# Routing of the second expert layer issued in two steps, its results scaled in a fixed place, and a table preload in one norm: a sequence model of four layers on one core

## The chip, the cores and the metric

One Trainium2 chip, of which the program uses one core. The metric is the time on the device in microseconds (us) for one execution of the whole program. The kernel before took 1866.34 us, the median of three runs (1865.36 to 1867.81).

## The reference

The input is x, 8 sequences of 256 tokens with 128 channels. Four layers, each with a token mixer and a feed-forward part, each followed by a residual and a layer norm:

- layer 0: a gated linear recurrence, then two blocks of local attention;
- layer 1: a selective state-space scan, then 32 experts, of which each token takes one;
- layer 2: two rounds of 16-head attention over chunks of each sequence, each with a small feed-forward part, then 8 experts, of which each token takes two, beside a common expert that all tokens take;
- layer 3: 16-head causal attention with a decay, then a linear layer with ternary weights.

The change touches the expert part of layer 2 and its seams to what stands before and behind it. Its reference, shortened:

```python
logits = rmsnorm(x) @ router_w.T
probs = softmax(logits)
topk_p, topk_i = top_k(probs, 2)
rw = topk_p / sum(topk_p)                      # gates of a token's two experts
sel = one_hot(topk_i, E).sum(1)
...                                            # first 320 tokens of each expert, in token order
gate = silu(einsum('ech,ehi->eci', xg, rg))
up = einsum('ech,ehi->eci', xg, ru)
eout = einsum('eci,eih->ech', gate * up, rd)   # weighted by rw and added back to the tokens
...
shared = silu(x @ sg) * (x @ su) @ sd          # the common expert, 1024 wide
return shared + routed
```

Behind it stands x = layernorm(x + that).

## The kernel before

Activations lie with the 128 channels on the partitions and the 2048 tokens along the free axis. The program is a row of stages: rglru, local_mamba, moe1, chunked, moe2, typed. Nearly every product goes through one helper, `mm`, so TensorE's instructions in the profile mostly name L394, and one has to tell them apart by their tiles.

**chunked** (L1343) computes the attention of layer 2. Each of the 8 sequences is a generator, `one_sequence` (L1394), that issues a piece of work and yields two guesses: how long TensorE will be busy with it, and how long its results then take. `on_pe` (L277) keeps three such generators alive and always continues the one whose guess says that it is ready first. So the order in which instructions are written is that of this small planner; it is fixed when the program is built, and each engine runs its own instructions in that order (the framework may still move an instruction ahead of others of its engine where nothing forbids it; `issue_after`, L396, fixes an order without adding a wait). The products of a stream carry the names kps (keys), vps (values), sc (scores), pt (transposed scores) and out.

At its end each sequence computes its logits lg for 8 experts and calls `route2` (L1014). This takes Ln and Exp for the norm's factor (L1024, L1025); finds the two best experts with VectorE's compares and maxima (L1030 to L1042, result sel); counts on TensorE, in products named cum, how many earlier tokens chose the same expert (with msk, a triangle of ones, and onesb, all ones); turns counts into places (L1050 to L1056); writes the token's row to its two places in DRAM by four indirect DMAs on GpSimd (`scatter`, L1081, issue at L1083); and computes the gates from an Exp of the difference of the two maxima (L1074 to L1079).

**moe2** (L1460) begins with `rows_of` (L1097): five loads of the placed rows from DRAM, on the queues of SyncE and ScalarE, each behind all scatters. Then comes `shared(0)`, the common expert for the first 512 tokens: eight chunks of a gate product pg, an up product pu, Silu (L1485), a multiplication on VectorE (L1486, tile sh) and a down product that adds to acc. pg and pu share two PSUM banks, sh has two buffers. The rows are transposed (bt), and the 8 experts run over 320 places each; results go to DRAM (ybuf). 32 gathers (`gather`, L1115, issue at L1117) bring the two rows of every group of 128 tokens back; GpSimd issues them. `results(b)` (L1523) weighs them with their gates (two operations on VectorE per group, L1529 and L1530), transposes them, adds the common expert's part and runs the layer norm. The calls stand as follows: shared(1); then shared(2) and shared(3), and between their chunks results(0), the first inputs of typed, and results(1). The results of sequences 2 to 7 are written in typed.

**A layer norm** in steps (L426 to L456) takes a mean product, a subtraction, Square on ScalarE (L448), a variance product, Ln (L453), Exp (L454) and a multiplication. Silu, Ln and Exp need tables in ScalarE; `exp_ln` (L414) loads a table that serves Ln and Exp both. Where the program asks for nothing, the compiler puts a table load ahead of a function that the present table lacks.

**typed** (L1697) runs the attention of layer 3 over 48 units, six per sequence; a queue `side` holds work to be put between units: the inputs of later sequences, their results, and the norms and linear layer behind the attention. Its softmax (L1650) is a maximum on VectorE (L1656), Exp on ScalarE (L1661), a reciprocal (L1663) and a multiplication on GpSimd (L1664).

Of the kernel before, what the change touches and what calls it, by code (L numbers as in the profile page):

```python
# [15 lines left out]
AF = mybir.ActivationFunctionType  # L16
# [280 lines left out]
class _Kernel:  # L297
# [128 lines left out]
    def layernorm_steps(self, pool, src, dst, eps=EPS, tag="ln", steps=False):  # L426

        nc = self.nc
        n = src.shape[-1]
        if not steps and n <= S:  # L430

            ps = self.psum(name="ln")
            xc, var = ps[:, 0:n], ps[:, S : S + n]
            self.mm(xc, self.centre, src)
            sq = pool.tile([P, n], F32, tag=tag + "sq", name="ln_sq", bufs=2)
            nc.scalar.activation(sq, xc, AF.Square)
            self.mm(var, self.mean, sq)
            rs = pool.tile([P, n], F32, tag=tag + "rs", name="ln_rs", bufs=2)
            nc.scalar.activation(rs, var, AF.Ln, bias=eps)
            nc.scalar.activation(rs, rs, AF.Exp, scale=-0.5)  # L440
            nc.vector.tensor_mul(dst, xc, rs)
            return
        mean = self.psum(name="ln_mean")[:, :n]
        self.mm(mean, self.mean, src)
        xc = pool.tile([P, n], F32, tag=tag + "xc", name="ln_xc")
        nc.vector.tensor_sub(xc, src, mean)
        sq = pool.tile([P, n], F32, tag=tag + "sq", name="ln_sq")
        nc.scalar.activation(sq, xc, AF.Square)  # L448
        yield
        var = self.psum(name="ln_var")[:, :n]  # L450
        self.mm(var, self.mean, sq)
        rs = pool.tile([P, n], F32, tag=tag + "rs", name="ln_rs")
        nc.scalar.activation(rs, var, AF.Ln, bias=eps)  # L453
        nc.scalar.activation(rs, rs, AF.Exp, scale=-0.5)  # L454
        yield
        nc.vector.tensor_mul(dst, xc, rs)  # L456

# [556 lines left out]
    def route2(self, b, z, work, small):  # L1014


        nc = self.nc
        E, CAP = 8, 320
        ts = slice(2 * b, 2 * b + 2)
        lg = self.lg2[:, ts]  # L1020
        four = small.tile([P, 7, 2, 2], F32, tag="four", name="four", bufs=2)
        mx, ix, sl, pos, sc, ok = (four[:, i] for i in range(6))
        rs = four[:, 6, 0]
        nc.scalar.activation(rs, self.ssq[:, ts], AF.Ln, scale=1.0 / P, bias=float(np.finfo(np.float32).eps))  # L1024
        nc.scalar.activation(rs, rs, AF.Exp, scale=-0.5)  # L1025
        shp = [P, 2, E]
        each = lambda a: a.unsqueeze(2).to_broadcast(shp)
        io = self.c("iota8").unsqueeze(1).to_broadcast(shp)
        oh = small.tile([P, 2, 2, E], F32, tag="oh", name="oh", bufs=2)
        nc.vector.tensor_tensor(lg, lg, each(rs), ALU.mult)  # L1030
        for k in range(2):

            o = oh[:, k]
            nc.vector.tensor_reduce(mx[:, k], lg, AX.X, ALU.max)
            nc.vector.tensor_tensor(o, lg, each(mx[:, k]), ALU.is_equal)
            nc.vector.tensor_tensor(o, o, io, ALU.mult)
            nc.vector.tensor_reduce(ix[:, k], o, AX.X, ALU.min)
            nc.vector.tensor_tensor(o, io, each(ix[:, k]), ALU.is_equal)
            if k == 0:
                nc.vector.scalar_tensor_tensor(lg, o, NEG, lg, ALU.mult, ALU.add)  # L1040
        sel = small.tile([P, 2, E], BF, tag="sel", name="sel", bufs=2)
        nc.vector.tensor_tensor(sel, oh[:, 0], oh[:, 1], ALU.add)  # L1042

        cum = self.psum("M", "cum")[:, 0 : 2 * E].rearrange("p (t e) -> p t e", e=E)
        self.mm(cum, self.m("upto"), sel, True, False)
        if b:
            self.mm(cum, self.onesb, self.sum2.unsqueeze(1).to_broadcast(shp), False, False)
        self.mm(cum[:, 1, :], self.onesb, sel[:, 0, :], False, True)
        nc.vector.tensor_scalar(sl, ix, float(CAP), float(E * CAP - 1), ALU.mult, ALU.add)
        nc.vector.tensor_tensor(oh, oh, cum.unsqueeze(1).to_broadcast([P, 2, 2, E]), ALU.mult)  # L1050
        nc.vector.tensor_reduce(pos, oh, AX.X, ALU.add)

        nc.vector.tensor_scalar(sc, pos, float(CAP), 100000.0, ALU.is_gt, ALU.mult)
        nc.vector.tensor_add(sl, sl, pos)
        nc.vector.tensor_add(sc, sc, sl)
        placed = nc.vector.tensor_copy(self.put2[:, :, ts], sc)  # L1056
        for t in range(2):
            for k in range(2):
                self.scatter(1, z[:, t, :], self.put2[:, k, 2 * b + t : 2 * b + t + 1])
        if b < B - 1:  # L1060
            with nc.allow_low_precision("whole numbers to 16"):
                for t in range(2):
                    if b or t:
                        nc.vector.tensor_add(self.sum2, self.sum2, sel[:, t, :])
                    else:
                        nc.vector.tensor_copy(self.sum2, sel[:, t, :])

        i = nc.vector.tensor_scalar(sl, sl, float(E * CAP - 1), None, ALU.min)
        self.issue_after([i], placed)
        nc.vector.tensor_copy(self.get2[:, :, ts], sl)  # L1070
        nc.vector.tensor_scalar(ok, pos, float(CAP), None, ALU.is_le)
        g = self.gate2[:, :, ts]
        nc.vector.tensor_sub(sc[:, 1], mx[:, 1], mx[:, 0])
        nc.scalar.activation(sc[:, 1], sc[:, 1], AF.Exp)  # L1074
        nc.vector.tensor_scalar(sc[:, 0], sc[:, 1], 1.0, None, ALU.add)
        nc.vector.reciprocal(sc[:, 0], sc[:, 0])
        nc.vector.tensor_mul(g[:, 0], sc[:, 0], ok[:, 0])
        nc.vector.tensor_mul(sc[:, 1], sc[:, 1], sc[:, 0])
        nc.vector.tensor_mul(g[:, 1], sc[:, 1], ok[:, 1])  # L1079
# [263 lines left out]
    def chunked(self):  # L1343
# [7 lines left out]
        with (  # L1351
# [42 lines left out]
            def one_sequence(b):  # L1394
# [35 lines left out]
                self.logits(b, y, self.w1[:, 866:874], self.lg2[:, 2 * b : 2 * b + 2, :])  # L1430
                assert self.routed == b
                self.routed = b + 1
                self.route2(b, z, work, small)
                yield 0.3, 0.0

            self.routed = 0
            on_pe([one_sequence(b) for b in range(B)], 3, [self.typed_weights(prep)])
# [22 lines left out]
    def moe2(self):  # L1460
# [9 lines left out]
        with (  # L1470
            tc.tile_pool(reuse_waits="tile", name="m2", bufs=1) as one,
            tc.tile_pool(reuse_waits="tile", name="m2w", bufs=2) as work,
        ):
            bt, group = self.rows_of(one, 1)
            ss = []

            def shared(i):
                cs = bass.ts(i, 512)
                acc = self.psum("S", "acc")
                for c in range(8):  # L1480
                    pg, pu = self.psum("A", "pg"), self.psum("A", "pu")
                    self.mm(pg, gu[:, 0, c * P : (c + 1) * P], x[:, cs])
                    self.mm(pu, gu[:, 1, c * P : (c + 1) * P], x[:, cs])
                    h = work.tile([P, 512], F32, tag="sh", name="sh")
                    nc.scalar.activation(h, pg, AF.Silu)  # L1485
                    nc.vector.tensor_mul(h, h, pu)  # L1486
                    self.mm(acc, down[:, c * P : (c + 1) * P], h, c == 0, c == 7)
                    yield
                s = keep.tile([P, 512], F32, name=f"s{i}")
                nc.vector.tensor_add(s, acc, x[:, cs])  # L1490
                ss.append(s)


            for _ in shared(0):
                pass
            ybuf = self.dram.tile([E * CAP, P], F32, name="ybuf2")
            groups = 0
# [25 lines left out]
            def results(b, work):  # L1523

                ps = self.psum("M", "back")
                for j in range(2):
                    t = 2 * b + j
                    r1, r2 = got[t]
                    nc.vector.tensor_scalar(r1, r1, self.gate2[:, 0, t : t + 1], None, ALU.mult)  # L1529
                    nc.vector.scalar_tensor_tensor(r1, r2, self.gate2[:, 1, t : t + 1], r1, ALU.mult, ALU.add)  # L1530
                    nc.tensor.transpose(ps[:, j * P : (j + 1) * P], r1, self.ident)
                s = work.tile([P, S], F32, tag="s", name="s")
                nc.vector.tensor_add(s, ss[b // 2][:, b % 2 * S : (b % 2 + 1) * S], ps[:, 0:S])
                yield
                yield from self.layernorm_steps(work, s, y[:, bass.ts(b, S)], steps=True)

            self.results = results
            for _ in shared(1):
                pass
            self.x = y  # L1540
            first = chain(results(0, self.ty), self.typed_before(0), results(1, self.ty))
            for i in (2, 3):
                for _ in shared(i):
                    next(first, None)
            for _ in first:
                pass
            self.exp_ln()


    def ternary_weights(self, pool, out):  # L1550
# [99 lines left out]
    def typed_softmax(self, unit, sc, work, small):  # L1650
# [9 lines left out]
        for i in reversed(range(n)):  # L1660
            nc.scalar.activation(e[:, i, :], sc[:, i, :], AF.Exp, bias=nm[:, i : i + 1], accum_out=sm[:, i : i + 1])  # L1661
        rc = small.tile([P, n], F32, tag="rc", name="rc")
        nc.vector.reciprocal(rc, sm)  # L1663
        nc.gpsimd.tensor_tensor(e, e, rc.unsqueeze(2).to_broadcast([P, n, keys]), ALU.mult)  # L1664
        return e

# [30 lines left out]
    def typed(self):  # L1697
# [21 lines left out]

        units = [(b, u) for b in range(B) for u in [(0, 0, 4), (0, 4, 8)] + [(1, r, r + 2) for r in range(0, 8, 2)]]  # L1720
        n = len(units)
        side = deque([before(1)])
        scs, es, o = {}, {}, None


# [66 lines left out]
```

## Time and profile before

| | |
|---|---|
| median of three runs | 1866.34 us |
| the profiled execution | 1891.69 us |
| its span, first to last instruction | 1889.9 us |
| mean granted TensorE clock | 0.916 of full |
| TensorE busy | 1575.9 us |
| VectorE busy | 1089.7 us |
| ScalarE busy | 1029.9 us |
| GpSimd busy | 564.0 us |

The profiled execution is 25.35 us above the median of the others. The stages that matter here, on the axis of its span: chunked's sequences up to about 1440 us, shared(0) from 1443 us, the experts, the gathers from 1539.7 to 1579.5 us, shared(2) and (3) from 1584.6 to 1634.5 us, and typed from 1635 us to the end.

How to read the lines. A group or timeline line names the source line, the engine, the operation, the tiles (output, then inputs), the shapes and how many instructions; then come busy time and mean ns in a group, or start and duration in us in a timeline. The bracket at the end of a timeline line is how long the engine had been idle before the instruction, and what ended that. "remote" or "another core or an unknown queue" means that no recorded event was found that ended the wait. Products are pipelined and their ends are modelled.

Two rows of slices, each 1/40 of the span, give the picture: the busy tenths of TensorE and its granted clock.

```profile
PE   3678877888888767677679999999987987999997
PEclk7789999989998898788789999999997998999999
```

A slice is 47.2 us. Counted from 1, slice 31 (1417 to 1465 us) holds the end of chunked and the start of shared(0), slice 34 (1559 to 1606 us) the end of the gathers; both stand at 7.

### The profile page before, as it was taken

To read this page: it belongs to the slowest core of one execution; us is meant where nothing else is said; L and a number is where in the kernel's file an instruction comes from. 1 tells how busy PE (TensorE), PEld (TensorE's weight loads), DVE (VectorE), ACT (ScalarE), POOL (GpSimd) and SP (SyncE) were. 2 spreads that over 40 slices of the span, in tenths; PEclk is the share of its full clock that TensorE was granted. 3 is DMA by queue.
4 is the path that set the end of the run, shared out by engine and by line. 5 is a ranking of instruction groups with operands and counts; after the bars stand their busy time and mean duration, and the time that the engine had idled before them with its cause. 6 is when DMAs were issued, how large, how long until landed. Compare 5 with 4: busy or idle time off the path is not lost.

```text
span 1889.9 us, 28445 instructions
## 1 busy us (share of the span) xinstructions
PE 1575.9 (83%) x10810; PEld 950.7 (50%) x10810; DVE 1089.7 (58%) x2018; ACT 1029.9 (54%) x2703; POOL 564.0 (30%) x493
## 2 busy tenths in 40 slices
PE   3678877888888767677679999999987987999997
PEld 2344544544454434344456676665653643466564
DVE  5734567786878686688434544457543223466664
ACT  4557777776876876455135444444432222466654
POOL 1324452515261413311320201111111034255462
PEclk7789999989998898788789999999997998999999
DMA  4000012121212122175410000000101210000000
GB/s 173 1 1 1 1 35 56 35 56 35 56 35 56 35 56 58 43 224 167 134 48 2 8 6 7 6 5 5 36 2 29 81 52 24 1 4 4 7 4 9
DMA packets 58330, 75.51 MB, mean 40 GB/s; under 512 B 5869, under 2 KB 35237, under 8 KB 57169
## 3 DMA queue, kind: packets, MB, share of 16 engines
q1 hardware_dynamic: 52864, 67.57, 12.3%
q0 software_dynamic: 3216, 5.07, 0.9%
q8 instruction: 85, 1.39, 0.3%
q10 hardware_dynamic: 2112, 1.05, 0.2%
q14 instruction: 53, 0.43, 0.1%
HBM read 65.46 MB, written 9.71 MB: 40 GB/s over the span
## 4 chain that ended last, share of the span: by engine, by line
PE 52%; DVE 18%; ACT 11%; POOL 7%; issue 7%; DMA 3%; another core or an unknown queue 1%; SPq 0%; POOLq 0%; DVEq 0%; ACTq 0%
PE sc L394 7%; PE vps L394 6%; PE kps L394 5%; PE pt L475 4%; PE out L394 4%; DVE hs L789 3%; PE o L394 3%; ACT e L647 3%; PE pu L394 3%; PE pg L394 3%; DVE hs L790 2%; DVE hs L787 2%; PE y L394 2%; PE hps L394 2%; PE py L394 2%
## 5 line engine op out<-in xcount | busy, mean ns | idle before, releaser
L394 PE MATMUL y<-hs,ident 128*128 128x512 f32 x256 | 148.1, 709 | 40.6 <-DVE hs L790 40.6
L789 DVE TENSOR_TENSOR_SCAN hs<-da,hs 128x1024 f32<-128x1024 f32 x64 | 148.8, 2334 | 3.8 <-ACT da L785 3.3
L475 PE MATMUL pt<-ident,e 128*128 128x128 f32 x768 | 125.0, 289 | 28.3 <-POOL e L652 18.1
L1661 ACT ACTIVATE e<-sc,nm 128x128 f32<-128x128 f32 (+1 forms) x256 | 104.3, 425 | 60.4 <-DVE nm L1656 59.7
L652 POOL TENSOR_TENSOR e<-e,rc 128x1024 f32<-128x1024 f32 x32 | 72.2, 2255 | 203.4 <-DVE rc L651 203.3
L785 ACT ACTIVATE da<-d,na 128x255 f32<-128x255 f32 x256 | 112.4, 504 | 36.7 <-DVE hs L789 19.3
L647 ACT ACTIVATE e<-sc,nm,rn 128x128 f32<-128x128 f32 x256 | 113.5, 464 | 25.1 <-DVE nm L642 25.0
L475 PEld LDWEIGHTS pt<-ident,e 128*128 128x128 f32 x768 | 89.7, 146 | 73.6 <-POOL e L652 25.3
L1293 POOL TENSOR_TENSOR e<-e,rc 128x512 f32<-128x512 f32 x32 | 33.6, 1051 | 303.8 <-DVE rc L1292 181.0
L1664 POOL TENSOR_TENSOR e<-e,rc 128x1024 f32<-128x1024 f32 x48 | 91.5, 1908 | 89.0 <-DVE rc L1663 86.1
L599 POOL TENSOR_TENSOR t<-t,t 128x512 f32<-128x512 f32 x64 | 89.1, 1392 | 95.3 <-DVE t L586 86.7
L787 DVE TENSOR_TENSOR hs<-u,bc 128x1024 f32<-128x1024 f32 x64 | 87.0, 1368 | 41.3 <-POOL u L774 26.2
L394 PEld LDWEIGHTS y<-hs,ident 128*128 128x128 f32 x256 | 52.3, 220 | 96.7 <-DVE hs L790 53.5
L477 ACT COPY ptsb<-pt 128x512 f32<-128x512 f32 x87 | 51.1, 588 | 90.7 <-PE pt L475 70.7
L1268 ACT COPY kp<-kps 128x512 f32<-128x512 f32 x128 | 74.8, 586 | 41.3 <-PE kps L394 39.8
L1117 POOL DMA_INDIRECT got<-ybuf,get x48 | 45.6, 951 | 166.1 <-DMA ybuf<-ys 117.0
L477 DVE COPY ptsb<-pt 128x512 f32<-128x512 f32 x105 | 70.4, 685 | 32.6 <-PE pt L475 32.4
L394 PE MATMUL qk<-w_local,h 128*128 128x512 f32 x128 | 71.8, 649 | 17.8 <-DVE t L586 13.0
L790 DVE TENSOR_TENSOR hs<-hs,bc 128x1024 f32<-128x1024 f32 x64 | 82.0, 1289 | 0.2
L1656 DVE TENSOR_REDUCE nm<-sc 128x4 f32<-128x1024 f32 (+1 forms) x48 | 58.4, 1217 | 31.8 <-PE sc L394 31.7
L1241 DVE BATCH_NORM_STATS2 st<-out 128x6 f32<-128x128 f32 x80 | 20.0, 289 | 91.6 <-PE out L394 84.3
L1304 ACT COPY vs<-vps 128x512 f32<-128x512 f32 x64 | 37.4, 585 | 59.6 <-PE vps L394 51.1
(387 smaller groups left out, 3903.8 us busy)
## 6 DMA issues: line engine op xcount, KB each, us to landing
bc<-xs SPq DMA_DIRECT2D x128, 256.0 KB
w_attn<-in_w_dram SPq DMA_DIRECT2D x4, 1024.0 KB
w_local<-in_w_dram SPq DMA_DIRECT2D x2, 1557.0 KB
places<-zeros SPq DMA_DIRECT2D x2, 1280.0 KB
w_moe<-in_e1gate_dram SPq DMA_DIRECT2D x8, 256.0 KB
w_moe<-in_e1up_dram SPq DMA_DIRECT2D x8, 256.0 KB
w_moe<-in_e1down_dram SPq DMA_DIRECT2D x8, 256.0 KB
w_moe<-in_e2rg_dram SPq DMA_DIRECT2D x8, 256.0 KB
```

The lines of the kernel that those rows point to most:

```text
L394: return self.nc.tensor.matmul(out, lhsT, rhs, start=start, stop=stop)
L475: self.last = self.nc.tensor.transpose(pt[:, j * P : (j + 1) * P], src[:, j * P : (j + 1) * P], self.ident)
L477: self.nc.any.tensor_copy(sb.rearrange("p a b -> p (a b)"), pt)
L599: nc.gpsimd.tensor_add(t1, t1, t2)
L647: nc.scalar.activation(e[:, j, g, :], scs[:, j, g, :], AF.Exp, bias=nm[:, j, g : g + 1], scale=rq[:, j, g : g + 1], accum_out=sm[:, j, g : ...
L785: nc.scalar.activation(da[:, n, c, 1:S], d[:, c, 1:S], AF.Exp, scale=na[:, i : i + 1])
L787: nc.vector.tensor_tensor(hs, u.unsqueeze(1).to_broadcast(shp), bn, ALU.mult)
L789: nc.vector.tensor_tensor_scan(line(hs), line(da), line(hs), 0.0, ALU.mult, ALU.add)
L790: nc.vector.tensor_tensor(hs, hs, cn, ALU.mult)
L1268: nc.scalar.copy(k[:, 2 * i : 2 * i + 2, :].rearrange("p a b -> p (a b)"), ps)
L1661: nc.scalar.activation(e[:, i, :], sc[:, i, :], AF.Exp, bias=nm[:, i : i + 1], accum_out=sm[:, i : i + 1])
L1664: nc.gpsimd.tensor_tensor(e, e, rc.unsqueeze(2).to_broadcast([P, n, keys]), ALU.mult)
```

## The change

Three things are changed.

First, `route2` becomes a generator. It stops behind sel, ahead of the count products, with a guess of 5 us until it can go on. In sequences 0 to 6 the planner puts other streams' pieces there; in the last sequence the second half is called from moe2, behind two chunks of shared(0), and the loads of the rows (`rows_of`) come behind that.

Second, the first scaling of each group of results must be issued behind the common expert's last multiplication that has been written by then, or, in typed, behind the last reciprocal of a softmax (`self.paced`). results(1) leaves moe2 and becomes the first thing in typed's `side`.

Third, in results(0) the table for Ln and Exp is loaded ahead of the norm, behind the last Silu written by then (`self.silu`), and the Silu that is written next behind the norm is issued behind the norm's Exp (`self.norm`). The load at the end of moe2 is tied to the last Silu as well.

```diff
@@ layernorm_steps
-        nc.scalar.activation(rs, rs, AF.Exp, scale=-0.5)
+        self.norm = nc.scalar.activation(rs, rs, AF.Exp, scale=-0.5)
@@ route2
         nc.vector.tensor_tensor(sel, oh[:, 0], oh[:, 1], ALU.add)
+        yield 0.0, 5.0
 
         cum = self.psum("M", "cum")[:, 0 : 2 * E].rearrange("p (t e) -> p t e", e=E)
@@ chunked, one_sequence
-                self.route2(b, z, work, small)
-                yield 0.3, 0.0
+                self.rest = self.route2(b, z, work, small)
+                yield 0.3, 1.0
+                if b < B - 1:
+                    yield from self.rest
+                else:
+
+                    next(self.rest)
@@ moe2
-            bt, group = self.rows_of(one, 1)
...
-                    nc.scalar.activation(h, pg, AF.Silu)
-                    nc.vector.tensor_mul(h, h, pu)
+                    i = nc.scalar.activation(h, pg, AF.Silu)
+                    if self.norm:
+
+                        self.issue_after([i], self.norm)
+                        self.norm = None
+                    self.silu = i
+                    self.paced = nc.vector.tensor_mul(h, h, pu)
...
-            for _ in shared(0):
+            self.norm = None
+            common = shared(0)
+            for _ in range(2):
+                next(common)
+            for _ in self.rest:
+                pass
+            bt, group = self.rows_of(one, 1)
+            for _ in common:
                 pass
@@ moe2, results
-                    nc.vector.tensor_scalar(r1, r1, self.gate2[:, 0, t : t + 1], None, ALU.mult)
+
+                    i = nc.vector.tensor_scalar(r1, r1, self.gate2[:, 0, t : t + 1], None, ALU.mult)
+                    self.issue_after([i], self.paced)
...
                 yield
+                if b == 0:
+                    self.exp_ln(self.silu)
                 yield from self.layernorm_steps(work, s, y[:, bass.ts(b, S)], steps=True)
...
-            first = chain(results(0, self.ty), self.typed_before(0), results(1, self.ty))
+            first = chain(results(0, self.ty), self.typed_before(0))
...
-            self.exp_ln()
+            self.exp_ln(self.silu)
@@ typed_softmax
-        nc.vector.reciprocal(rc, sm)
+        self.paced = nc.vector.reciprocal(rc, sm)
@@ typed
-        side = deque([before(1)])
+        side = deque([chain(self.results(1, work), before(1))])
```

## The prediction

> **What bounds the kernel now.** I read the engine totals first, then the chain of work that ended last by engine and line, then the groups of instructions, and then timelines and stage windows around the places that the change touches. The totals make TensorE the bound on average (busy 83% of the span). The chain says where it is not:
>
> ```profile
> PE 1575.9 (83%) x10810; PEld 950.7 (50%) x10810; DVE 1089.7 (58%) x2018; ACT 1029.9 (54%) x2703; POOL 564.0 (30%) x493
> PE 52%; DVE 18%; ACT 11%; POOL 7%; issue 7%; DMA 3%; another core or an unknown queue 1%; SPq 0%; POOLq 0%; DVEq 0%; ACTq 0%
> L1117 POOL DMA_INDIRECT got<-ybuf,get x48 | 45.6, 951 | 166.1 <-DMA ybuf<-ys 117.0
> ```
>
> The gathers of the routed rows (L1117) should not matter: TensorE has shared(1) to do meanwhile. The stage windows (columns: start and end, length, then busy time of PE, PEld, DVE, ACT and POOL, granted clock, DMA share, GB/s) show that they do:
>
> ```profile
> 1539.00:1576.00 37.00, 25.74 (x43) 9.59 (x41) 12.79 (x34) 3.58 (x6) 27.49 (x29) 0.82 0.17 50
> 1576.00:1582.50 6.50, 0.00 (x0) 0.00 (x0) 0.84 (x2) 0.00 (x0) 2.84 (x3) 0.63 0.14 40
> 1600.00:1636.00 36.00, 33.65 (x82) 13.71 (x83) 11.83 (x22) 14.10 (x19) 5.16 (x4) 1.00 0.00 0
> 1636.00:1890.00 254.00, 242.32 (x1752) 145.98 (x1748) 153.46 (x279) 146.08 (x607) 127.28 (x76) 0.98 0.02 5
> ```
>
> In the first two TensorE is neither full nor at full clock; from 1600 it is 93 to 95% busy. VectorE's timeline says why:
>
> ```profile
> 1543.50 0.35 DVE L1530 SCALAR_TENSOR_TENSOR got<-got,gate 128x128 f32<-128x128 f32 x1 [1.00 <-DMA got<-ybuf,get]
> 1549.93 0.67 DVE L1486 TENSOR_TENSOR sh<-sh,pu 128x512 f32<-128x512 f32 x1
> 1576.04 0.35 DVE L1530 SCALAR_TENSOR_TENSOR got<-got,gate 128x128 f32<-128x128 f32 x1 [1.02 <-DMA got<-ybuf,get]
> 1582.01 0.69 DVE L1486 TENSOR_TENSOR sh<-sh,pu 128x512 f32<-128x512 f32 x1 [5.62 <-remote]
> ```
>
> All 32 scalings (L1529 and L1530) stand in VectorE's queue among the gate products of shared(1) (L1486), each behind its own gather; one gather leaves GpSimd every 1.25 us. So a gate product, and the down projection behind it, moves at the pace of the gathers.
>
> **Part two, the scalings behind the gate products.** Gate products of shared(1) start at 1537.39, 1540.23, then 1543.77 ... 1582.01. Where nothing disturbs them (shared(0), 1455.97 to 1458.81) they stand 2.83 us apart. Seven such steps from 1537.39 give 1557.2, against 1582.01: 24.8 us are lost. Of these 5.6 stand in the row with the releaser "remote": VectorE was free at 1576.4, and TensorE's signal came late. Rows like it stand wherever scatters or gathers are in flight (next part) and sum to about 19 us in this execution. It took 1891.69 us (span 1889.9), 25.35 more than the median of the three timed runs, 1866.34, so I suspect that such late signals are largely absent from timed runs. I count only what the queue explains: 24.8 - 5.6 = 19.2. Bounds 15 (if four scalings still meet a late gather) and 24.8.
>
> What is late next? POOL ends its gathers at 1579.5 as before. With shared(1) done near 1559, shared(2) and (3) run under the gathers and end some 50 us later, so the last rows are long there; the first sequence's four rows land by 1546. POOL's q, k and km (L1609, L1616) of typed's first unit queue behind the gathers, and are wanted only then too.
>
> The 28 scalings of sequences 1 to 7 are issued in typed, 4 per sequence at 0.31 to 0.35 us: 1.3 us each, 9 in all, on a VectorE that is busy 153 of 254 us while TensorE is at 95%. Mostly hidden, but they delay the maxima and copies TensorE waits for: +1, bounds 0 and +9. The norm of sequence 1 moves into typed as well: TensorE work 0.38 + 0.43 + 0.43 = 1.24 us leaves one dense stage for another, zero (bounds 0 and +3).
>
> **Part one, the routing in two steps.** For the last sequence nothing else is queued on TensorE:
>
> ```profile
> 1442.90 0.17 PE L394 MATMUL cum<-sel,msk 128*128 128x16 bf16 x1 [3.03 <-DVE sel L1042]
> 1443.41 2.08 PE L394 MATMUL pg<-x_chunked,w_shared 128*128 128x512 f32 x2 [0.28 <-DVE oh L1050]
> 1444.47 0.20 ACT L1074 ACTIVATE four<-four 128x2 f32<-128x2 f32 x1 [5.64 <-DVE four L1073]
> 1444.69 1.28 ACT L1485 ACT_TABLE_LOAD   x1
> ```
>
> In the order of the changed kernel a first pg and pu (2.08 + 1.92 at the low clock) stand ahead of cum, and the silu table is loaded right behind the exponentials. They fill the wait of 3.03 us and the 0.28 behind it. The clock matters here. "TensorE: Matmul & The Clock Gate" of the Trainium skill (What's actually happening) has the full clock return after about 3.4 us of sustained work. The row shows 2.08 us for a pair that takes 1.02 later. By the row alone the gain is 3.3; by the rule the earlier work also brings the clock back about one pair sooner, some 4.3. Against it: the gate's exponential (L1074) now comes after two silus and brings two loads of its own, 2.57 us plus 0.2, where a chunk leaves ScalarE 2.83 - 0.60 = 2.2 free: +0.5. Sum -3, bounds -4.3 and 0. Its four scatters and the loads of places behind them on SP's and ACT's queues go up to 1 to 2 us later; their rows are transposed at 1467.04, where the trace shows no wait, and loads issued at 1450.6 leave over 9 us.
>
> For sequences 0 to 6 cum moves behind some 27 more vps (or kps) products:
>
> ```profile
>   DVE sel L1042: 5.6, 7
> ```
>
> This line of cum's own view (idle us of TensorE, times) is 3.03 for the last sequence, so only 2.6 for all others; up to 2.6 is won, I take -2. The scatters go about 3 to 6 us later and now lie beside pt and out rather than beside vps. Sequence 6 shows what that can cost:
>
> ```profile
> 1088.19 0.59 ACT L477 COPY ptsb<-pt 128x512 f32<-128x512 f32 x1 [4.37 <-remote]
> 1418.55 0.59 ACT L477 COPY ptsb<-pt 128x512 f32<-128x512 f32 x1 [5.65 <-remote]
> ```
>
> In sequence 0 TensorE's signal came 1.65 us later than its product ended, in sequence 6, where pt was issued 1.2 us after the first scatter, 4.32 us; each is released 5.8 us after the first scatter. If the change makes sequences 0 to 5 like 6, that is up to 2.7 x 6 = 16 us in such an execution. Since I hold these late signals to be weak in timed runs, I put +1 (bounds 0 and +16).
>
> **Part three, one table for the norm.** ScalarE's order in the changed kernel reads: table, square, silu table, silu, table, Ln, table, Exp, silu table. The preload is undone by the silu between, so Ln and Exp still load one each. For the one norm left: loads and Ln and Exp without a silu between are 3 x 1.283 + 0.39 + 0.42 = 4.7 us between two silus, against 2.83 per chunk: TensorE waits about 1.9. The square between two loads is 2 x 1.283 + 0.42 = 3.0: about 0.5. Before, a silu stood between Ln and Exp in both norms, and the chunks grew by about 0.5 each: 1.0. Here the skill speaks against the change: "ScalarE: Activation LUTs" (What ACT_TABLE_LOAD costs) prices a switch at 2.66 us, load and drain. By the rule the gap is 3 x 2.66 + 0.81 = 8.8 and the wait 6. The trace has no drain: Ln ends at 1593.71 and the next load starts at 1593.72. I use the rows: 2.4 - 1.0 = +1.5, bounds 0 and +6.
>
> **Sum.** -19.2 + 1 - 3 - 2 + 1 + 1.5 = -20.7. On the median, 1866.3 - 20.7 = 1845.6; on the profiled execution, 1891.7 - 20.7 - 5.6 (its late signal) = 1865.4.
>
> **The rivals.**
> 1. Cleaner than I think: the whole 24.8 goes and routing gives its full 4.3 + 2.6, scalings free: 1866.3 - 24.8 - 6.9 + 1.5 = 1836. For it: VectorE idles 40% in typed. Against: the last 5.6 is a signal, not a queue.
> 2. The gain is partly paid back in typed: the scalings lie ahead of the maxima (L1656) that release typed's exponentials, and cost their whole 9 us and 3 for the norm: 1845.6 + 8 + 3 = 1857. For it: TensorE there has 12 us of slack in 254. Against: only 1.3 us at a time.
> 3. Slower: scatters beside pt. One place, one price: in each of sequences 0 to 5 TensorE's signal waits out the whole 5.8 us from the first scatter, 4.3 us more than now and in timed runs as well; with the half clock after such an idle stretch (0.5 in the trace at 1417 to 1431) some 4.5: 6 x 4.5 = 27, hence 1845.6 - 1 + 27 = 1872. It decides from 3.5 us per sequence (21 / 6) on. Against: odd sequences still have 12 vps products behind cum.
> 4. No change in the end: the gathers bind anyway, because shared(2) or typed's start waits for POOL. Then 19 is lost again: 1865. Against: 50 us of products stand between.
>
> **How the numbers follow.** My forecast has 0.58, rival 1 0.14, rival 2 0.14, rival 3 0.08, rival 4 0.06. The range, 1834 to 1860, takes in the forecast's own bounds and the first two rivals. Timing of this kernel can tell 0.2%, 3.7 us, from no change. Faster than 1862.6: 0.58 + 0.14 + 0.14 and a third of rival 4, 0.88; within 0.2%: 0.04; slower: 0.08.
>
> **What would show it.** Gate products of shared(1) 2.83 us apart and shared(1) over near 1559; TensorE over 90% busy at full clock between 1539 and 1576 of the old axis; pg right behind lg at the last sequence; five loads in the norm and a silu gap near 4.7 us; scatters 3 to 6 us later in sequences 0 to 5 and the waits with "remote" behind them no longer than now. I am wrong if those grow beyond 3.5 us each, if a gate product still waits for a gather, or if typed's stage grows by more than 4 us over its 254.

## The result, and the profile after

The changed kernel takes 1847.85 us, the median of four runs (1847.43 to 1852.0), against 1867.07 us of the kernel before in the same rounds (four runs, 1865.36 to 1867.89): a ratio of 0.9903, 95% interval 0.9886 to 0.992. So it is 19.2 us faster there. On one other chip, where the last two experiments ran, it was 12.5 us slower; the section behind the experiments is about that.

The page of the changed kernel, totals, chain and the group of gathers:

```profile
PE 1557.4 (84%) x10810; PEld 942.1 (51%) x10810; DVE 1095.6 (59%) x2016; ACT 1028.5 (56%) x2704; POOL 563.7 (30%) x493
PE 54%; DVE 19%; ACT 13%; issue 6%; POOL 6%; DMA 2%; POOLq 0%; DVEq 0%; SPq 0%; ACTq 0%
L1118 POOL DMA_INDIRECT got<-ybuf,get x48 | 45.7, 951 | 157.5 <-DMA ybuf<-ys 116.5
```

The gathers cost GpSimd what they did, and "another core or an unknown queue" has left the chain. The stage windows (columns as in the prediction) of the changed kernel, first the gathers from the issue of the first to the end of the last, then typed from its first scores to its last linear product:

```profile
1512.80:1552.60 39.80, 38.57 (x92) 15.87 (x91) 13.05 (x25) 15.40 (x21) 30.31 (x32) 1.00 0.20 52
1582.46:1840.80 258.34, 246.35 (x1753) 147.56 (x1753) 168.96 (x301) 146.22 (x609) 127.84 (x76) 0.98 0.02 5
```

The same two of the kernel before, from a second profile of it (run before_again below), since its first was out of the ordinary:

```profile
1520.20:1559.90 39.70, 26.77 (x45) 9.85 (x45) 14.20 (x38) 4.18 (x7) 30.25 (x32) 0.80 0.19 51
1610.82:1854.90 244.08, 238.16 (x1747) 144.42 (x1747) 152.07 (x276) 144.80 (x604) 127.20 (x76) 1.00 0.02 5
```

Beside the gathers TensorE now runs 92 products at full clock instead of 45 at 0.80. But typed has grown by 14.2 us, and VectorE's busy time in it by 16.9. VectorE's timeline around the end of shared(1), changed kernel:

```profile
1527.55 0.69 DVE L1496 TENSOR_TENSOR sh<-sh,pu 128x512 f32<-128x512 f32 x1 [2.15 <-PE pu L394]
1530.38 0.69 DVE L1496 TENSOR_TENSOR sh<-sh,pu 128x512 f32<-128x512 f32 x1 [2.15 <-PE pu L394]
1533.82 0.47 DVE L1547 TENSOR_SCALAR got<-got,gate 128x128 f32<-128x128 f32 x2
1534.21 0.60 DVE L1549 SCALAR_TENSOR_TENSOR got<-got,gate 128x128 f32<-128x128 f32 x2
```

The gate products stand 2.83 us apart and the first scalings come behind shared(2)'s first, without a wait for a gather.

Where the time went, by stage, in us between the starts of products (the profile's spans; ahead of the first lg, where the change does not reach, these two runs differ by 3.8 us):

| stage | before, second profile | changed kernel | difference |
|---|---|---|---|
| first to last sequence's logits (lg) | 344.9 | 336.2 | -8.7 |
| last lg to typed's first scores (sc) | 191.4 | 168.0 | -23.4 |
| first sc to the last linear product | 244.1 | 258.3 | +14.2 |
| sum | 780.4 | 762.5 | -17.9 |

The -23.4 of the middle row can be followed in the gate products: -22.0 in shared(1) and the step behind it, -2.2 between the last lg and the end of shared(0), and +1.0 in shared(2) and (3); the rest lies in the experts.

### The profile page after: what moved, and what is told of

The parts are those of the page before. It is cut to its first block, busy times and chain, and to the rows that moved or that the text cites. A ratio compares the mean times of both kernels' runs of the same rounds, so it can differ in the third digit from the quotient of the medians.

```text
span 1850.2 us, 28438 instructions
## 1 busy us (share of the span) xinstructions
PE 1557.4 (84%) x10810; PEld 942.1 (51%) x10810; DVE 1095.6 (59%) x2016; ACT 1028.5 (56%) x2704; POOL 563.7 (30%) x493
## 4 chain that ended last, share of the span: by engine, by line
PE 54%; DVE 19%; ACT 13%; issue 6%; POOL 6%; DMA 2%; POOLq 0%; DVEq 0%; SPq 0%; ACTq 0%
PE vps L394 7%; PE sc L394 7%; PE kps L394 6%; DVE hs L789 4%; PE out L394 4%; PE pt L475 4%; PE o L394 3%; PE pu L394 3%; PE pg L394 3%; ACT e L647 3%; DVE hs L790 2%; DVE hs L787 2%; PE y L394 2%; PE acc L394 2%; PE py L394 2%
## 5 line engine op out<-in xcount | busy, mean ns | idle before, releaser
L394 PE MATMUL sc<-km,q 64*128 64x512 f32 x192 | 69.9, 648 | 1.7 <-DVE FunctionType.Silu _12235 L1500 0.9
```

The lines of the kernel that those rows point to most:

```text
L394: return self.nc.tensor.matmul(out, lhsT, rhs, start=start, stop=stop)
```

## The experiments

Times are medians; "before" is the kernel before in the same rounds. The first eight runs were made on one chip, before_again and last_whole on a second, the last two on a third; for the changed kernel's own 1847.85 us the chip is not known. Before takes 1865.06 to 1868.39 us on the first two, so a difference of 2 or 3 us between medians of different rounds says little, and the stages of the profiles are used for such sizes.

**only_route**: part one alone on the kernel before (route2 as a generator, the last sequence's second half and the loads of the rows in shared(0); nothing else).

> Only part one: the routing in two steps, the rest as before. Theory of the forecast: the last sequence's filled wait (-3), the other sequences' waits for sel (-2) and nothing lost at the scatters: 4 to 5 us under before (1867), about 1862.5. Rival, that the late signals near the scatters (some 13 us of waits at ptsb, and vps products slowed in the profile of before) are part of timed runs too and go when cum moves: 12 to 20 us under before, about 1850. In the profile the last logits product would come about 337 us after the first in both cases if the late signals go, 355 to 365 if they stay.

1856.95 us against 1865.06, ratio 0.9959 (0.9947 to 0.9972): 8 us faster, twice the forecast and short of the rival. First to last lg took 336.1 us.

**only_results**: part two alone.

```diff
-                    nc.vector.tensor_mul(h, h, pu)
+                    self.paced = nc.vector.tensor_mul(h, h, pu)
...
+                    self.issue_after([i], self.paced)
...
-            first = chain(results(0, self.ty), self.typed_before(0), results(1, self.ty))
+            first = chain(results(0, self.ty), self.typed_before(0))
...
-        nc.vector.reciprocal(rc, sm)
+        self.paced = nc.vector.reciprocal(rc, sm)
...
-        side = deque([before(1)])
+        side = deque([chain(self.results(1, work), before(1))])
```

> Only part two: scalings behind the common expert's products, sequence 1's result moved into typed. By the forecast: -19.2 in shared(1), +1 in typed: about 1849. Rival from the trace of after, where typed is 12.7 us longer from its first scores to its last linear product: -19.2 - 1.3 + 12.7 = -8, about 1859. The gate products of shared(1) should stand 2.83 us apart in both.

1857.2 us, ratio 0.9962 (0.9949 to 0.9975): the rival's -8. First to last lg took 345.0 us with the old order of cum and without one late signal, so the 8.9 us between these two runs is what the moved count products are worth. PE's rows show how the forecast saw only a third of it. Sequence 2 here (timeline of TensorE, only_results):

```profile
1185.62 1.02 PE L394 MATMUL vps<-sa_vp,x_lf 128*32 128x512 f32 x2
1186.88 0.17 PE L394 MATMUL cum<-sel,msk 128*128 128x16 bf16 x1 [0.23 <-DVE sel L1042]
1187.02 3.21 PE L394 MATMUL vps<-sa_vp,x_lf 128*32 128x512 f32 x27
```

and in only_route:

```profile
1184.36 3.62 PE L394 MATMUL vps<-sa_vp,x_lf 128*32 128x512 f32 x32
1190.49 0.18 PE L394 MATMUL cum<-sel,msk 128*128 128x16 bf16 x1
```

Thirty-two vps products take 3.62 us, 0.11 each, yet two of them ahead of cum are drawn as 1.02. A product's row runs to its modelled end, which lies far behind the moment when the next could start: the second of the two starts at 1186.05 and cum at 1186.88, 0.83 us apart, and the bracket shows 0.23 of that. So a wait for sel is hidden in the row ahead of it. The whole wait is read from the distance of products on both sides of it: from lg to pt this sequence takes 11.66 us in only_results and 10.32 in only_route, 1.34 us, and 8.9 / 7 is 1.27. How the 1.34 us divide among the products between lg and pt is not shown.

**no_table**: the changed kernel without its third part.

```diff
-                    if self.norm:
-
-                        self.issue_after([i], self.norm)
-                        self.norm = None
...
-                if b == 0:
-                    self.exp_ln(self.silu)
...
-            self.exp_ln(self.silu)
+            self.exp_ln()
```

> The changed kernel without part three (no preload in the first norm, no Silu tied behind the norm's Exp). By the forecast the tables cost 1.5 us net over the old order, so 2 to 3 us faster than the changed kernel, about 1845.5. Rival, that the tie saves loads: slower than it by 1 to 2 us. The gap of 4.73 us between two Silus should be gone, with a Silu between Ln and Exp instead.

1845.59 us, ratio 0.9897 (0.9883 to 0.9911). That is 2.3 us under the changed kernel's median, but before was lower by 2.0 in these rounds too; what holds is the 1.8 us less from the last lg to the first sc (166.2 against 168.0). ScalarE's timeline in the changed kernel shows what the third part does:

```profile
1539.66 1.28 ACT L453 ACT_TABLE_LOAD   x1
1540.96 0.38 ACT L453 ACTIVATE ln_rs<-ln_var 128x256 f32<-128x256 f32 x1
1541.36 1.28 ACT L454 ACT_TABLE_LOAD   x1
1543.09 1.28 ACT L1490 ACT_TABLE_LOAD   x1
1544.38 0.60 ACT L1490 ACTIVATE sh<-pg 128x512 f32<-128x512 f32 x1
```

Ln and Exp each still load a table, and no Silu stands between them: 4.73 us from the end of one Silu (1539.65) to the start of the next. In no_table one stands there:

```profile
1535.18 0.38 ACT L453 ACTIVATE ln_rs<-ln_var 128x256 f32<-128x256 f32 x1
1535.58 1.28 ACT L1490 ACT_TABLE_LOAD   x1
1536.87 0.60 ACT L1490 ACTIVATE sh<-pg 128x512 f32<-128x512 f32 x1
1537.49 1.28 ACT L454 ACT_TABLE_LOAD   x1
```

**results1_back**: the changed kernel with sequence 1's result in moe2 again.

```diff
-            first = chain(results(0, self.ty), self.typed_before(0))
+            first = chain(results(0, self.ty), self.typed_before(0), results(1, self.ty))
...
-        side = deque([chain(self.results(1, work), before(1))])
+        side = deque([before(1)])
```

> The changed kernel with sequence 1's result back in moe2, its scalings still behind the gate products. Theory: in typed the inputs of sequence 1 wait for its result and norm, which costs some 5 us at typed's start; back in moe2 the norm costs 1.3 us of products and 1 to 4 us of tables: 0 to 3 us faster than the changed kernel, about 1846, with pt of the first unit about 10.6 us behind the first scores instead of 15.8. Rival, that typed grows by the scalings alone: 1 to 4 us slower, about 1850, and typed as long as in the changed kernel.

1850.93 us, ratio 0.9927 (0.9914 to 0.994), with runs from 1847.21 to 1854.88: not faster, as the theory had it, but 3.1 us slower by the medians, the rival's figure. Of the mechanism half holds, against the rival: the first pt comes 9.4 us behind the first sc instead of 15.8, and typed is 252.8 us instead of 258.3. But a second norm with the closed table gap costs 7.0 us in moe2 (175.0 against 168.0), more than the 2.3 to 5.3 that I allowed (1.3 for products, 1 to 4 for tables).

**scale_early**: the scalings of sequences 1 to 7 in shared(3).

```diff
...
+            later = list(range(1, B))
             for i in (2, 3):
                 for _ in shared(i):
                     next(first, None)
+                    if i == 3 and later:
+                        scale(later.pop(0))
```

> The changed kernel with the 28 scalings of sequences 1 to 7 put behind the gate products of shared(3), four each, where VectorE is free for 2.15 us per chunk. In the changed kernel typed repeats every 31.60 us per sequence, before it was 30.69. Theory: the scalings in typed cost that 0.9 us per sequence, so typed returns to 30.7 and the kernel gains 6 to 7 us: about 1841. Rival of the forecast, that they cost about 1 us in all and the 0.9 us come from elsewhere: 1847, period stays 31.6.

1841.15 us against 1866.63, ratio 0.9868 (0.9852 to 0.9883): 6.7 us under the changed kernel's median. The period of typed is 30.69 us again, and typed takes 250.5 us: the scalings cost it 7.8. In shared(3) they cost nothing: the gate products still stand 2.83 us apart, and from the last lg to the first sc it is 168.0 us as in the changed kernel.

```profile
1561.06 0.69 DVE L1496 TENSOR_TENSOR sh<-sh,pu 128x512 f32<-128x512 f32 x1 [1.23 <-PE pu L394]
1561.67 0.48 DVE L1545 TENSOR_SCALAR got<-got,gate 128x128 f32<-128x128 f32 x2
1562.06 0.60 DVE L1547 SCALAR_TENSOR_TENSOR got<-got,gate 128x128 f32<-128x128 f32 x2
1563.90 0.69 DVE L1496 TENSOR_TENSOR sh<-sh,pu 128x512 f32<-128x512 f32 x1 [1.23 <-PE pu L394]
```

**best_tight** and **best_split**: both with sequence 1's result in moe2 and the scalings of 2 to 7 in shared(3). best_tight is to put the preload behind the norm's Square, best_split leaves out the third part. The piece of best_tight that differs in the tables:

```diff
-                if b == 0:
-                    self.exp_ln(self.silu)
-                yield from self.layernorm_steps(work, s, y[:, bass.ts(b, S)], steps=True)
+                steps = self.layernorm_steps(work, s, y[:, bass.ts(b, S)], steps=True)
+                next(steps)
+                yield
+                if b < 2:
+                    self.exp_ln(self.silu)
+                yield from steps
```

> The changed kernel with sequence 1's result back in moe2, the scalings of sequences 2 to 7 in shared(3), and both norms of moe2 with one table load ahead of Ln and Exp together and one back to Silu (two loads instead of five). Theory: typed as before (first pt 9.4 us behind the first scores, period 30.7, 245 us to the last linear product against 258), the norms cost 1.2 to 2 us each: 1836 to 1838. Rival, that the two norms with a closed gap cost as much as sequence 1's result in typed: 1841 or more.

> As the tight one, but with the tables left to the compiler (a Silu between Ln and Exp, four loads per norm). By the table counts: two gaps of 2.95 us between Silus, each 0.7 us over the usual 2.24, so 1.4 us per norm; the tight form has one gap of 3.4 us, 1.2 over. So the two within 1 us of each other. Rival, that the count of loads decides (8 against 4, 1.28 us each): the split one is 3 to 5 us slower.

1837.84 us (ratio 0.9844, 0.9828 to 0.9859) and 1835.25 us (ratio 0.9839, 0.9825 to 0.9852). Both beat the kernel before and the changed one; typed takes 244.3 and 244.6 us, as before the change. Their intervals overlap; by the stage from the last lg to the first sc the split form is 3.7 us shorter. So the count of loads does not decide, as the rival had it, and "within 1 us" holds for the first norm alone: over it the gate products stand 3.14, 3.31 and 3.69 us apart in the tight form and 2.99, 3.34 and 3.80 in the split one. In the second, the tight form's load stands ahead of the Square, not behind it, and the distances 5.11 and 4.67 stand against 3.26 and 2.84.

**route_last_only**: the changed kernel with sequences 0 to 6 routed in one piece.

```diff
-                yield 0.3, 1.0
                 if b < B - 1:
-                    yield from self.rest
+                    for _ in self.rest:
+                        pass
...
+                yield 0.3, 0.0
```

> The changed kernel with the routing of sequences 0 to 6 in one piece as before and only the last sequence's in two steps. The traces of the runs with the old and the new place of cum differ by 8.9 us between the first and the last logits product (345.0 and 336.1), without any late signal in either. Theory: the wait for sel is 1.3 us per sequence, of which the rows show only 0.2 to 0.7 because the product ahead of it is drawn to its modelled end: 8 to 9 us slower than the changed kernel, about 1856.5, and 345 us. By the forecast's row (2.6 us in all): 2 to 3 us slower, about 1850.

1858.13 us, ratio 0.9956 (0.9943 to 0.997), 10.3 us above the changed kernel's median, and 345.0 us from first to last lg. By the stage it is the theory's figure; by the medians a little more, and far from the forecast's 2 to 3.

**before_again** and **last_whole** (no_table with the last sequence's routing in one piece too).

> The kernel before, unchanged, profiled once more. Theory: the late signals of TensorE in its first profile (13 us of waits in chunked and 5.6 in shared(1)) belong to that one execution: this one takes about 1866 us, with 345 us between the first and the last logits product, no wait with the releaser remote, and typed at 245.6 us. Rival, that they come with this kernel's order: near 1890 and 364 us.

> The changed kernel without part three (1845.6 us by itself) and with the last sequence's routing in one piece ahead of shared(0), as before; sequences 0 to 6 stay in two steps. Theory of the forecast: the wait of 3.03 us for sel comes back, less 0.5 for the two table loads: 2 to 3 us slower, about 1848.5. Rival, that the waits of the Silus on the loads of the rows and on the gate's exponential take the gain back: 0 to 1 us slower.

before_again took 1865.9 us, with 344.9 us for the sequences, 244.1 for typed and no wait with the releaser "remote". last_whole took 1848.5 us (1844.43 to 1850.27; ratio 0.9894, 0.9876 to 0.9912) and 168.1 us from the last lg to the first sc, against 1845.59 and 166.2 of no_table. The last sequence's second step is worth 1.9 us by the stage. The medians cannot tell: the two kernels ran on different chips, and against before in their own rounds they have the same ratio (0.9894 and 0.9897).

**behind_max** and **after_again**: the changed kernel with typed's scalings tied to the maximum, and the changed kernel as it is.

```diff
-        nc.vector.tensor_reduce(nm, sc, AX.X, ALU.max, negate=True)
+        self.paced = nc.vector.tensor_reduce(nm, sc, AX.X, ALU.max, negate=True)
...
-        self.paced = nc.vector.reciprocal(rc, sm)
+        nc.vector.reciprocal(rc, sm)
```

> The changed kernel with the scalings of typed tied behind the last maximum (the reduction that gives nm) instead of behind the last reciprocal. In the changed kernel the reciprocal releases GpSimd's multiplication of e, and the weighted sums that follow it on VectorE take 1161 ns on the mean (1.98 us where they meet it, 0.34 where they don't). Theory: VectorE stands still while GpSimd holds what both need, so out of GpSimd's way the sums take about 0.35 us and the period per sequence goes from 31.60 to at most 31.2: 2 to 4 us faster than the changed kernel. Rival, that the four instructions themselves are the cost: the period stays at 31.6.

> The changed kernel once more, unchanged, on the chip and in the rounds of the run above: 1847 to 1848, period 31.60.

These two ran on a chip where the kernel before takes 1890.27 us (13 runs, 1885.94 to 1897.14), about what its first profiled execution took. behind_max took 1899.63 us (ratio 1.0045, 1.0026 to 1.0065), after_again 1902.76 us (ratio 1.0066, 1.005 to 1.0083). So the expectation of 1847 for the changed kernel is missed by 55 us, and on this chip the change is slower by 12.5.

For the scalings the comparison holds within the pair. VectorE's groups over 140 us of typed, after_again and then behind_max:

```profile
L1549 DVE SCALAR_TENSOR_TENSOR got<-got,gate 128x128 f32<-128x128 f32 x8 | 9.0, 1162 | 0.0
```

```profile
L1549 DVE SCALAR_TENSOR_TENSOR got<-got,gate 128x128 f32<-128x128 f32 x8 | 2.7, 341 | 0.0
```

The period goes from 31.60 to 30.55 us, and typed, in one profile of each, from 260.4 to 252.2. The medians differ by 3.1 us and their intervals overlap, so how much of the 8 us in the stage reaches the whole is not settled. But the same instructions stand in typed in both runs: the price was not the instructions but where they stood.

## On one chip, the other sign

TensorE's timeline in after_again during the gathers:

```profile
1558.16 1.02 PE L394 MATMUL pu<-x_chunked,w_shared 128*128 128x512 f32 x2
1560.59 1.12 PE L394 MATMUL pg<-x_chunked,w_shared 128*128 128x512 f32 x2 [1.40 <-issue]
1570.57 2.08 PE L394 MATMUL acc<-sh,w_shared 128*128 128x512 f32 x2 [8.86 <-issue]
1572.44 0.63 PE L1550 MATMUL back<-ident,got 128*128 128x128 f32 x2
1572.87 1.60 PE L394 MATMUL pu<-x_chunked,w_shared 128*128 128x512 f32 x2
1582.17 1.22 PE L394 MATMUL ln_mean<-s,mean 128*128 128x256 f32 x2 [7.70 <-DVE s L1552]
```

The brackets say that TensorE stood still for 8.9 and 7.7 us, and no scaling stands in the way there. Its signals reach the other engines late, VectorE's in the same run:

```profile
1569.83 0.69 DVE L1496 TENSOR_TENSOR sh<-sh,pu 128x512 f32<-128x512 f32 x1 [4.92 <-remote]
1581.69 0.42 DVE L1552 TENSOR_TENSOR s<-FunctionType.Silu _11529,back 128x256 f32<-128x256 f32 x1 [10.26 <-remote]
```

The multiplication at 1569.83 takes a pu product whose row ends at 1559.18, and VectorE had been free for 4.9 us; the one at 1581.69 takes back, whose products end at 1573.07, 8.6 us earlier.

Such waits stand in this run and in behind_max beside five of the eight groups of scatters and in the gathers. Of the other twelve profiles only the first of the kernel before has them. It is not known on which chip that one was taken; its 1891.69 us fit this chip's 1890.27, and it shares another trait with the two runs here alone: in these three traces no DMA has a landing time, while each of the other eleven has one for 128 of 345 DMAs. So that its late signals belong to the chip, and not to the one execution, is likely but not shown.

By stage, that first profile against after_again: 364.7 and 366.4 us for the sequences, 196.5 and 190.3 to the first sc, 245.6 and 260.4 for typed. If the first may stand for this chip, the moved count products gain nothing here instead of 8.9, of the 23 us in moe2 6 are left, and typed costs its 14 as everywhere, which gives the sign. What makes TensorE's signals late is open: it comes while indirect DMAs of GpSimd are under way, and no experiment separated these from anything else on that chip. Nor is it shown how many chips are like it, nor what scale_early or best_split would take there.

## Why the prediction was right, and where it was not

The total, -20.7 against -19.2 measured, is right by luck: by stage the forecast was -1 for the sequences, -20.7 from the last lg to the first sc and +1 for typed, and -8.7, -23.4 and +14.2 were measured. Two gains that were too small cancel a loss that was taken at next to nothing. By a sign that the prediction had itself set, typed growing by more than 4 us, its account of typed was wrong.

- **The scalings in shared(1).** -19.2. Right in mechanism and size: the seven steps took 38.95 us in before_again (1517.90 to 1556.85) and take 19.83, so 19.1 are won. An eighth, into shared(2), was left out: 5.74 against 2.83 us, another 2.9.
- **The last sequence's wait.** -3. Right in kind and within its bounds: 1.9 by last_whole. Of the two sums for the clock the row's held, not the one with the rule: after the change the pairs at the low clock are as many as before (2.08, 1.91 and 1.42 us in the changed kernel, 2.07, 1.91 and 1.41 in before_again), and the second pg starts 3.1 us sooner behind lg, not 4.3.

```profile
1415.75 2.08 PE L394 MATMUL pg<-x_chunked,w_shared 128*128 128x512 f32 x2 [0.27 <-DVE lg L816]
1417.62 1.91 PE L394 MATMUL pu<-x_chunked,w_shared 128*128 128x512 f32 x2
1419.45 1.42 PE L394 MATMUL pg<-x_chunked,w_shared 128*128 128x512 f32 x2
```

- **The count products of sequences 0 to 6.** Mis-sized: -2 taken, -8.9 measured. The step that failed is "so only 2.6 for all others": idle time read from the bracket of a row whose predecessor is drawn to a modelled end. The +1 for scatters beside pt did not show on the first two chips, where no signal is late.
- **Typed.** The step that failed is "Mostly hidden": +1 taken for the scalings, and zero for the norm of sequence 1. They cost 7.8 us (scale_early) and 5.5 (results1_back), both gone in best_split. That is about the size of the second rival, 9 and 3, but not by its reason, which was their own 0.3 us each. The durations of 0.31 to 0.35 us came from a stretch in which GpSimd computed nothing. In typed the changed kernel ties the scalings to the reciprocal, and that same reciprocal releases GpSimd's multiplication of e (timeline, changed kernel; the last two rows are from the next unit):

```profile
1604.27 1.90 POOL L1685 TENSOR_TENSOR e<-e,rc 128x1024 f32<-128x1024 f32 x1 [0.79 <-DVE rc L1684]
1604.28 1.97 DVE L1547 TENSOR_SCALAR got<-got,gate 128x128 f32<-128x128 f32 x1
1608.46 1.90 POOL L1685 TENSOR_TENSOR e<-e,rc 128x1024 f32<-128x1024 f32 x1 [2.30 <-DVE rc L1684]
1608.67 1.23 DVE L1677 TENSOR_REDUCE nm<-sc 128x4 f32<-128x1024 f32 x1 [0.29 <-PE sc L394]
```

  The first two start together and end together. In each of the six sequences whose scalings run in typed, one of the four is stretched so, to 1.97 or 1.98 us. The maximum at 1608.67, which reads PSUM, is not: 1.23 us, its usual time. "SBUF — State Buffer" of the Trainium skill (SBUF: two separate sides) has a pair of ports that GpSimd shares with those VectorE operations that have two inputs in SBUF or run in a two-port mode; it is an exclusive lock, which the first to start holds for its whole instruction while the other stands still. The 1.97 us beside 1.90, against 0.26 to 0.28 for the same operation elsewhere in typed, agree, and behind_max takes the price away without taking an instruction away. The norm's 5.5 us go with a chain at typed's start: the inputs of sequence 1 wait for its result and norm, and the first pt comes 6.4 us later behind the first sc.
- **The tables.** +1.5 net forecast (its 2.4 - 1.0 is 1.4), +1.0 measured in shared(2) and (3), with all that the second norm took there gone. For the norm that stays, 2.4 - 0.5 = 1.9 was forecast and 1.8 measured, with the gap of 4.73 us between Silus against the 4.7 worked out. The loads stand 1.28 us long directly behind the instruction ahead, so the rows were the right source, and not the 2.66 us per switch that the prediction weighed against them.
- **The late signals.** "Largely absent from timed runs" held for the result and the first ten experiments and failed on the third chip. Their sum of "about 19" was too small. The chain of the first profile in order of time has five waits without a recorded releaser, 24.2 us in all, which is nearly the whole 25.35 by which that profile lay above the timed runs:

```profile
1083.82 4.35 another core or an unknown queue
1196.27 4.34 another core or an unknown queue
1309.90 4.33 another core or an unknown queue
1412.89 5.63 another core or an unknown queue
1576.40 5.53 another core or an unknown queue
```

  The rival on the slower side named 1872 by this mechanism. On the third chip the change was slower indeed, but not at that rival's place: if the first profile may stand for that chip, the sequences grew by 1.7 us, and it is typed with 14.8 that tips the sum.

## What to carry to other kernels

An idle time in front of a product says little when the row ahead is drawn to its modelled end: measure the distance between two products that bracket the wait. An instruction is costed from a row in which the other engines do what they will do at its new place, and "behind X" is a poor place for it when X also starts GpSimd. Work put into the idle slots of VectorE in shared(3) cost nothing, and the same work in typed, behind the reciprocal, cost 7.8 us. And a total that comes out right says nothing of its terms until each stage has been measured by itself.

## What had not been expected of the hardware

The same program took 1866 us on some chips and 1890 on another, in every run there, and a change of 1% had the opposite sign on the two. The difference shows as signals of TensorE that come 8 us late and more while scatters and gathers are under way.
